# A two-layer graph network on one core: the gathers without memsets, comparisons and one-hot matrices in turn on VectorE, and the last table in four banks

## The chip, the core and the metric

The kernel runs on one core of a Trainium2 chip. Its engines are called by the profile's names: PE (TensorE, the matrix engine; PEld is its weight load), DVE (VectorE), ACT (ScalarE), POOL (GpSimd) and SP (SyncE). [...] An indirect DMA, which fetches rows by a list of indices, is issued by POOL.

The metric is device microseconds (us) of one execution, the median of the runs shown.

## The reference

`x` has 12500 nodes of 128 features. 200000 edges go from `src` to `dst`, sorted by `dst`, and each has one of 8 types. Two layers are computed, each of the form

```
W    = einsum("rb,bio->rio", comp, basis)        # one 128x128 matrix a type
msgs = einsum("ni,rio->nro", x, W)[src, et]      # a message an edge
mean = segment_sum(msgs, dst*8 + et) / max(count, 1)   # mean a node and type
h    = relu(mean.sum over types + x @ root + bias) + x
```

and the output is `layernorm(x + h)` after the second layer, row by row. All of it is float32.

## The kernel before, in words

**Tiles and batches.** The sorted edges are cut into 1563 tiles of 128 edges. Eight tiles make a batch (the code's `q`, `o` or `g`; 196 batches a layer, the last with 3 tiles). For every tile POOL issues one indirect gather (line 645) of 128 rows of 512 bytes: rows of `x` in the first layer (`l == 0`), rows of the table `y_d` in the second. The rows of a batch land in one of `AHEAD + 2` = 7 buffers (`rows_r`, line 556); gathers are issued 5 batches ahead of their use.

**First layer.** For each tile, `onehot` (line 964) writes a 128x128 matrix `dm` on DVE: 1/count where a column is the edge's place (node and type, `kr`), 0 elsewhere (line 979, 8 instructions a batch, which read `cols` in PSUM). `means` (line 1047) multiplies the gathered rows by `dm` on PE (line 1055); float32 matmuls appear twice in the profile, so a batch has 16. `take_means` copies the result to SBUF on ACT, `product` (line 1076) applies the 8 type matrices (line 1084), `place` (line 1096) adds the result to the right nodes by another one-hot matrix `pl` (made at the end of `onehot`, line 987), and `finish` (line 1123) adds bias and root term, the relu and the residual. Each finished block of 128 nodes is then multiplied by the second layer's type matrices (`table`, line 1163, two halves of four types each, bank `pt`) and stored to `y_d`. There are 98 such blocks. The second layer gathers from `y_d`, so it begins when the last table is stored.

**Preparation.** The indices and weights that `onehot` and the gathers use are made during the first 27 batches or so of the first layer, from the edge lists, in groups of four blocks of 128 tiles (`groups`, line 713; the first group is one block and is prepared before the loop). `counts` (line 786) is a generator whose steps are taken two a batch (line 1379): a key; then 47 comparisons of shifted keys on DVE (line 806, float16), four a step, each followed on PE by two counting matmuls into the bank `ct` (lines 812 and 813); then steps for `kr`, the reciprocal of the counts `w` (line 829), `idy` and `near`, each with transposes on PE. The comparisons write into two buffers `eq` in turn, four slots each; a buffer is free again when the counting matmuls that read it are done. `sources` (line 781) makes the gather indices of a later group. `where` (line 855) and checks of the input run in the same place of the loop.

**Order and waits.** `Plan.add` (line 326) takes each piece of work with the cells that it reads and writes, and each engine runs its pieces in the order in which they were added. A piece waits, before its first instruction, for all that its cells need, and its semaphore is raised by its last instruction. In the loop `plan.lazy` is set: a wait for another engine's piece is then moved to the next piece of that engine that already raises a semaphore, if there is one (lines 368 to 370); `means` always raises one (`plan.mark("PE")`).

**Pace of the gathers.** After each of the first 96 gathers POOL runs a memset of 128x256 floats (line 654), and before a memset it waits for the memset two before (line 653).

**End of the first layer.** After the loop the last batches are written out one by one (lines 1421 to 1462). A tile's last halves of tables alternate between `pt` and `ct` for the last two blocks.

Of the kernel before, what the change touches and what calls it, by code (L numbers as in the profile page):

```python
# [422 lines left out]
def ordered_path(  # L423
# [191 lines left out]

    rows_g = {}


    PACE = 2
    rest = keep([P, PACE, 256], F32, "rest")  # L620
    paced = tc.alloc_semaphore("s_paced")
    slow = [0]

    def slower(l, i):
        return 256 if l == 0 and i < 96 else 0

    def gather(l, q):
        if q >= NQ:
            return
        t, cell = rows_r.take()  # L630
        rows_g[l, q] = (t, cell)
        ids = idx if l == 0 else idy

        b = q * Q // P
        reads = [("idy" if l else "idx", b)]
        if l == 0 and q == 0:
            reads = [("idx0", 0), ("idx0", Q // 2)]
        if l == 1 and q == 0:
            reads += [("y_d", j) for j in range(NT - 2)] + [("y_d", j, k) for j in (NT - 2, NT - 1) for k in (0, 1)]

        def some(i0, i1):
            def emit():
                ins = []
                for i in range(i0, i1):
                    ins.append(nc.gpsimd.indirect_dma_start(  # L645
                        out=t[:, i - q * Q, :], out_offset=None, in_=x if l == 0 else y_d,
                        in_offset=bass.IndirectOffsetOnAxis(ap=ids[:, i:i + 1], axis=0)))
                    n = slower(l, i)
                    if n:
                        k = slow[0]  # L650
                        slow[0] += 1
                        if k >= PACE:
                            nc.gpsimd.wait_ge(paced, k - PACE + 1)
                        nc.gpsimd.memset(rest[:, k % PACE, :n], 0).then_inc(paced, 1)  # L654
                return ins

            return emit

        i0, n = q * Q, in_quad(q)
        after = [("done", l)] if q >= NQ - LATE else []  # L660
        if q == NQ - 2:
            for h in range(2):
                plan.add("POOL", some(i0 + h * 4, i0 + h * 4 + 4), reads, [cell + (h,)], lane="gq", n=4, after=after)
        else:
            plan.add("POOL", some(i0, i0 + n), reads, [cell + (0,), cell + (1,)], lane="gq", n=n, after=after)
# [117 lines left out]
        vec(lambda: nc.vector.tensor_copy(t[:, :b1 - b0, :], src_i[:, b0:b1, :]), ends("src", b0, b1), [c])  # L783
        turned("DVE", idx, "idx", t, c, b0, b1, Q if b0 == 0 else 0)

    def counts(i):


        b0, b1 = groups[i]
# [12 lines left out]
        for s0 in range(1, HALO, S4):  # L802
            ss = range(s0, min(s0 + S4, HALO))
            eq, ec = eqs.take()
            for s in ss:
                vec(lambda s=s, eq=eq, s0=s0: nc.vector.tensor_tensor(
                    eq[:, s - s0, :nb, HALO - s:HALO + P], key[:, :nb, HALO - s:HALO + P],
                    key[:, :nb, HALO:HALO + P + s], op=ALU.is_equal), ["key"], [ec + (s - s0,)])

            def emit(ss=ss, eq=eq, s0=s0):  # L810
                for s in ss:
                    nc.tensor.matmul(ct[:, :nb, :], id_h, eq[:, s - s0, :nb, main], start=(s == 1), stop=False)
                    last = nc.tensor.matmul(ct[:, :nb, :], id_h, eq[:, s - s0, :nb, HALO - s:HALO + P - s],
                                            start=False, stop=(s == HALO - 1))
                return last

            pe(emit, [ec + (s - s0,) for s in ss] + ["id_h"], [cc])
            yield
        rel, rc = turns.take()
        vec(lambda: nc.vector.tensor_tensor(rel[:, :nb], dx[:, bs, main],  # L820
# [143 lines left out]
    def onehot(l, q, g=None):  # L964

        if q >= NQ and (g is None or g < 0):
            return
        emits, reads, cells = [], ["cols"], []
        if q < NQ:
            if l == 0:  # L970
                t = dm_t[:, q % 4 // 2, :].rearrange("p (b t c) -> p b t c", b=2, t=Q)[:, q % 2]
                cells += [("dm", q % 4)]
            else:
                t = dm_t[:, q % 2, :].rearrange("p (t c) -> p t c", t=Q)
                cells += [("dm", 2 * (q % 2)), ("dm", 2 * (q % 2) + 1)]
            dms[l, q] = (t, list(cells))
            wide, ids = (P, kr) if l == 0 else (2 * P, near)
            for i in range(q * Q, q * Q + in_quad(q)):
                emits.append(lambda i=i: nc.vector.tensor_scalar(  # L979
                    t[:, i - q * Q, :wide], cols[:, :wide], ids[:, i:i + 1], w[:, i:i + 1], op0=ALU.is_equal,  # L980
                    op1=ALU.mult))
            b = q * Q // P
            reads += [("kr" if l == 0 else "near", b), ("wt", b)]
        if g is not None and g >= 0:
            m = tiles_of(g) * K
            o, c = pl[g] = pl_r.take()
            emits.append(lambda: nc.vector.tensor_scalar(  # L987
                o[:m], cols[:m], pos[:m, g // (2 * R), g % (2 * R):g % (2 * R) + 1], None, op0=ALU.is_equal))
            reads.append("pos")
            cells.append(c)  # L990

        vec(in_turn(emits), reads, cells)
        plan.mark("DVE")

# [49 lines left out]
    def two_blocks(g):  # L1044
        return (g + 1) // 2 - 1

    def means(o):
        t, c = rows_g.pop((0, o))
        d, dc = dms.pop((0, o))
        n = in_quad(o)  # L1050

        def some(i0, i1):
# [4 lines left out]

            return emit

        if o == NQ - 2:  # L1060
            for h in range(2):
                pe(some(4 * h, 4 * h + 4), [c + (h,)] + dc, [s_b[h][1], ("done", 0)])
# [4 lines left out]
    def take_means(o):  # L1067
        n = in_quad(o)
        t, c = sT[o] = sT_r.take()
        for h in range(-(-n // 4)):  # L1070
# [92 lines left out]
    def table(j):  # L1163
# [3 lines left out]
        split = j >= NT - 2  # L1167

        def half(k):
            hb, bc = ct_b if split and k == 1 else pt_b  # L1170

            def first_step():
                pe(lambda: nc.tensor.matmul(hb[:n].rearrange("p r d -> p (r d)"), hT[:, j * P:j * P + n],  # L1173
# [131 lines left out]
    for q in range(AHEAD):  # L1305
        gather(0, q)
    load_x(0)
    run(counts(0), 99)
    sources(*groups[1])
    for h in range(S // 4):  # L1310
        for step in turn_x(0, h):
# [49 lines left out]
    for o in range(NG - 3):  # L1361
# [2 lines left out]
        batch(o)  # L1364
        if o == 1:
            where()
        onehot(0, o + 2, o - 2)
        if not opened:
            end()
# [3 lines left out]
        if o > 0:  # L1373
# [2 lines left out]
                take_product(o - 1)  # L1376
            else:
                late_y.append(o - 1)
        for i in range(2):
            if parts is not None:  # L1380
                if run(parts, 1):
                    parts = None
            elif later:
                later.pop()()
        if o > 2:
            k = place(o - 3)
            close(k)
# [50 lines left out]
    onehot(0, NQ, g - 2)  # L1438
    product(g - 2)
    take_product(g - 2)  # L1440
    while tables:
        table_now()
    placed(g - 2)
    onehot(0, NQ, g - 1)
    onehot(0, NQ, g)
    means(g - 1)
    take_means(g - 1)
    means(g)
    take_means(g)
    product(g - 1)  # L1450
# [4 lines left out]
    placed(g)  # L1455
    now = tables[:]
    tables.clear()
    for h in (0, 2):
        for a, _ in now[h:h + 2]:
            a()  # L1460
        for _, b in now[h:h + 2]:
            b()

    for q in range(AHEAD):
        gather(1, q)
# [94 lines left out]
```

## Time and profile before

| | us |
|---|---|
| median of 3 runs | 3981.41 (3975.88 to 3983.71) |
| the profiled execution | 3979.88 |
| its span, from the first to the last instruction | 3978.1 |
| busy: PE, PEld | 2532.4, 2046.9 |
| busy: DVE, ACT | 1660.6, 390.6 |
| busy: POOL | 2997.6 |
| first gather of the first layer starts | 4.51 |
| first gather of the second layer starts | 2006.07 |
| last memset starts | 149.2 |

The busy times are sums over the whole span; engines work beside each other. POOL's idle time between two gathers stands as "issue" where no other engine ended it. A row of a timeline gives the start and the length of an instruction, or of several alike put together (x8), then the engine, the line, the operation, what it writes and reads, and in brackets how long the engine was idle before it and who ended that. PE's clock, as granted, is given as a share of full speed.

### The profile page before, as it was taken

What the parts mean: (1) busy time and instruction counts of PE and PEld (TensorE: products, weight loads), DVE (VectorE), ACT (ScalarE), POOL (GpSimd) and SP (SyncE); (2) the same over time, 40 slices, a digit from 0 to 9 for tenths busy, and PEclk for the clock granted to TensorE, in tenths of its full rate; (3) what the DMA queues carried; (4) which work ended last, traced back from release to release, by engine and by line L of the source; (5) the groups of instructions that cost most, each with busy time, mean ns of one, the idle gap of its engine ahead of it and who ended that gap; (6) DMA issues with size and microseconds to landing.
All of it is one profiled execution on the core that took longest, in us unless ns stands there. A gap on an engine that the chain in (4) does not pass through costs nothing.

```text
span 3978.1 us, 32124 instructions
## 1 busy us (share of the span) xinstructions
PE 2532.4 (64%) x11213; PEld 2046.9 (51%) x11213; DVE 1660.6 (42%) x4643; ACT 390.6 (10%) x838; POOL 2997.6 (75%) x3230
## 2 busy tenths in 40 slices
PE   6776677776666666667755566555555556555554
PEld 4655555555555555555544444444444444444443
DVE  6566333333333333333234444444444444444443
ACT  1111122221111111111200000000000000000000
POOL 8877777777777777777767777777777777777776
PEclk8897888888888888888877777777777777777777
DMA  3112233332222222222322222222222222222221
GB/s 117 48 52 69 64 106 101 106 95 80 85 85 79 86 85 77 82 80 90 95 68 53 63 53 63 53 64 63 53 63 64 53 63 53 63 64 53 63 58 52
DMA packets 129374, 284.55 MB, mean 72 GB/s; under 512 B 53920, under 2 KB 61356, under 8 KB 129204
## 3 DMA queue, kind: packets, MB, share of 16 engines
q0 software_dynamic: 100032, 205.07, 19.8%
q1 hardware_dynamic: 26122, 75.69, 5.1%
q8 instruction: 90, 1.47, 0.2%
q10 hardware_dynamic: 3049, 1.67, 0.2%
q14 instruction: 81, 0.66, 0.1%
HBM read 223.56 MB, written 58.65 MB: 71 GB/s over the span
## 4 chain that ended last, share of the span: by engine, by line
POOL 74%; issue 23%; PE 2%; DMA 1%; DVE 0%; POOLq 0%; ACT 0%; ACTq 0%; SPq 0%
POOL rows L645 73%; POOL rest L654 1%; PE s L1055 0%; DMA rows<-in_x_dram,idx 0%; PE y L1084 0%; PE pt L1173 0%; PE ct L1084 0%; POOLq L398 0%; PE s L1216 0%; PE po L1115 0%; DVE x_g L1275 0%; DMA y_d<-y_row 0%; DMA rows<-y_d,idy 0%; DMA idx<-in_src_dram 0%; ACT y_row L606 0%
## 5 line engine op out<-in xcount | busy, mean ns | idle before, releaser
L645 POOL DMA_INDIRECT rows<-y_d,idy x1563 | 1476.6, 945 | 495.1 <-issue 495.1
L645 POOL DMA_INDIRECT rows<-in_x_dram,idx x1563 | 1488.2, 952 | 465.0 <-issue 460.0
L979 DVE TENSOR_SCALAR dm<-cols,near,w 128x256 f32<-128x256 f32 x1563 | 724.0, 535 | 1091.5 <-PE s L1216 723.6
L1216 PE MATMUL s<-dm,rows 128*128 128x256 f32 x2086 | 736.7, 522 | 512.7 <-DMA rows<-y_d,idy 489.8
L1216 PEld LDWEIGHTS s<-dm,rows 128*128 128x128 f32 x2086 | 550.5, 274 | 665.6 <-DVE dm L979 268.7
L1055 PE MATMUL s<-dm,rows 128*128 128x128 f32 x3126 | 570.5, 357 | 497.6 <-DMA rows<-in_x_dram,idx 496.6
L1055 PEld LDWEIGHTS s<-dm,rows 128*128 128x128 f32 x3126 | 526.0, 262 | 625.1 <-DMA rows<-in_x_dram,idx 563.0
L979 DVE TENSOR_SCALAR dm<-cols,kr,w 128x128 f32<-128x128 f32 x1563 | 514.7, 401 | 635.9 <-PE s L1055 510.8
L1216 PE MATMUL ct<-dm,rows 128*128 128x256 f32 x1040 | 364.2, 519 | 266.5 <-DMA rows<-y_d,idy 247.5
L1216 PEld LDWEIGHTS ct<-dm,rows 128*128 128x128 f32 x1040 | 272.4, 272 | 342.6 <-issue 140.3
L1084 PE MATMUL y<-w_sb,sT 128*128 128x128 f32 x1824 | 269.7, 311 | 30.8 <-ACT sT L606 30.7
L1084 PEld LDWEIGHTS y<-w_sb,sT 128*128 128x128 f32 x1824 | 261.7, 228 | 37.2 <-ACT sT L606 36.7
L606 ACT ACTIVATE sT<-s 128x512 f32<-128x512 f32 x391 | 213.3, 606 | 204.4 <-PE s L1055 204.3
L1133 DVE TENSOR_TENSOR v<-po,carry 128x128 f32<-128x128 f32 x98 | 28.5, 290 | 483.5 <-PE s L1055 327.5
L606 ACT ACTIVATE y_row<-pt 128x512 f32<-128x512 f32 x196 | 117.1, 597 | 1136.9 <-PE s L1055 1037.0
L1173 PE MATMUL pt<-w_sb,arena 128*128 128x512 f32 x388 | 204.2, 608 | 35.0 <-ACT y_row L606 35.0
L1268 ACT ACTIVATE st<-st,eps 128x8 f32<-128x8 f32 (+1 forms) x13 | 4.0, 308 | 1958.5 <-DVE dm L979 1841.0
L1084 PE MATMUL ct<-w_sb,sT 128*128 128x128 f32 (+1 forms) x1312 | 191.6, 309 | 1.2 <-ACT sT L606 1.2
L1084 PEld LDWEIGHTS ct<-w_sb,sT 128*128 128x128 f32 (+1 forms) x1312 | 188.5, 228 | 1.5 <-ACT sT L606 1.4
L1115 PE MATMUL po<-pl,ys 128*128 128x256 f32 x392 | 117.7, 383 | 0.8 <-DVE pl L987 0.8
L1173 PEld LDWEIGHTS pt<-w_sb,arena 128*128 128x128 f32 x388 | 63.5, 190 | 81.5 <-ACT y_row L606 77.9
L987 DVE TENSOR_SCALAR pl<-cols,pos 128x256 f32<-128x256 f32 x196 | 92.4, 472 | 0.0
(135 smaller groups left out, 1008.0 us busy)
## 6 DMA issues: line engine op xcount, KB each, us to landing
y_d<-y_row SPq DMA_DIRECT2D x96, 512.0 KB, 2.8
rows<-in_x_dram,idx POOLq DMA_INDIRECT x1563, 2.5
rows<-y_d,idy POOLq DMA_INDIRECT x1563, 2.5
x_g<-in_x_dram SPq DMA_DIRECT2D x24, 512.0 KB, 4.6
out_dram<-x_g SPq DMA_DIRECT2D x12, 512.0 KB, 2.7
arena<-in_L_gnn_basis_dram SPq DMA_DIRECT2D x2, 512.0 KB
w_d<-y_row SPq DMA_DIRECT2D x2, 512.0 KB, 2.8
w_sb<-w_d SPq DMA_DIRECT2D x2, 512.0 KB
```

Of the source, the lines that this page charges most:

```text
L606: act(lambda: nc.scalar.activation(out_t, in_t, AF.Copy), reads, writes)
L645: ins.append(nc.gpsimd.indirect_dma_start(out=t[:, i - q * Q, :], out_offset=None, in_=x if l == 0 else y_d, in_offset=bass.IndirectOffset ...
L654: nc.gpsimd.memset(rest[:, k % PACE, :n], 0).then_inc(paced, 1)
L979: emits.append(lambda i=i: nc.vector.tensor_scalar(t[:, i - q * Q, :wide], cols[:, :wide], ids[:, i:i + 1], w[:, i:i + 1], op0=ALU.is_equa ...
L987: emits.append(lambda: nc.vector.tensor_scalar(o[:m], cols[:m], pos[:m, g // (2 * R), g % (2 * R):g % (2 * R) + 1], None, op0=ALU.is_equal))
L1055: last = nc.tensor.matmul(s_b[i // 4][0][:, i % 4, :], t[:, i, :], d[:, i, :], start=True, stop=True)
L1084: last = nc.tensor.matmul(y[:m], t[:, r, :nt, :].rearrange("p t k -> p (t k)"), w_sb[:, 0, r, :], start=(r == 0), stop=(r == R - 1))
L1115: ins = nc.tensor.matmul(a, o[:m], t[:m], start=opens, stop=last and not root_in)
L1133: emits.append(lambda: nc.vector.tensor_add(v[:, :n], a[:, :n], t[:, :n]))
L1173: pe(lambda: nc.tensor.matmul(hb[:n].rearrange("p r d -> p (r d)"), hT[:, j * P:j * P + n], w_sb[:, 1, k * H:(k + 1) * H, :].rearrange("p ...
L1216: ins = nc.tensor.matmul(a, t[:, i, :], d[:, i, :], start=(opens and i == 0), stop=(last and i == n - 1))
L1268: act(lambda: nc.scalar.activation(st[:p, :k, A + M], st[:p, :k, A + 1], AF.Sqrt, bias=eps[:p]), [sc + (1,), "eps"], [sc + (2,)])
```

## The change

Four things are changed, all in the first layer.

- The memsets between the first 96 gathers, their waits, their semaphore and their buffer are gone.
- `counts` no longer puts its comparisons and counting matmuls into the plan at once, but into the lists `between` and `behind` (the first group, prepared before the loop, still does). `onehot` takes the comparisons in `between` and sets each behind one of its own instructions, so that they alternate in one single piece of work of DVE. The counting matmuls in `behind` are added after `product`.
- For this the two preparation steps of a batch are taken ahead of `onehot`, no longer after `product`. The other steps (keys, `kr`, `w`, `idy`, `near`, `sources`, checks) move there as they are, with their transposes.
- At the end of the layer `means` and `take_means` of the last full batch can be done by halves, and a table is put between the halves; the last block's two table halves use the banks of `means` (`s_b`), so that the last two blocks have four banks, and their four matmuls are added before their four copies.

```
-                    n = slower(l, i)
-                    if n:
-                        k = slow[0]
-                        slow[0] += 1
-                        if k >= PACE:
-                            nc.gpsimd.wait_ge(paced, k - PACE + 1)
-                        nc.gpsimd.memset(rest[:, k % PACE, :n], 0).then_inc(paced, 1)
...
-    def counts(i):
+    between, behind = [], []
+
+    def counts(i, alone=False):
...
             for s in ss:
-                vec(lambda s=s, eq=eq, s0=s0: nc.vector.tensor_tensor(
+                one = (lambda s=s, eq=eq, s0=s0: nc.vector.tensor_tensor(
                     eq[:, s - s0, :nb, HALO - s:HALO + P], key[:, :nb, HALO - s:HALO + P],
                     key[:, :nb, HALO:HALO + P + s], op=ALU.is_equal), ["key"], [ec + (s - s0,)])
+                if alone:
+                    vec(*one)
+                else:
+                    between.append(one)
...
-            pe(emit, [ec + (s - s0,) for s in ss] + ["id_h"], [cc])
+            act_on = (emit, [ec + (s - s0,) for s in ss] + ["id_h"], [cc])
+            if alone:
+                pe(*act_on)
+            else:
+                behind.append(act_on)
...
+        for i, (e, r, c) in enumerate(between):
+            emits.insert(2 * i + 1, e)
+            reads += r
+            cells += c
+        between.clear()
         vec(in_turn(emits), reads, cells)
...
-            hb, bc = ct_b if split and k == 1 else pt_b
+            hb, bc = s_b[k] if j == NT - 1 else ct_b if split and k == 1 else pt_b
...
-    run(counts(0), 99)
+    run(counts(0, True), 99)
...
         batch(o)
         if o == 1:
             where()
+        for i in range(2):
+            if parts is not None:
+                if run(parts, 1):
+                    parts = None
+            elif later:
+                later.pop()()
         onehot(0, o + 2, o - 2)
...
-        for i in range(2):
-            if parts is not None:
-                if run(parts, 1):
-                    parts = None
-            elif later:
-                later.pop()()
+        for step in behind:
+            pe(*step)
+        behind.clear()
         if o > 2:
             k = place(o - 3)
...
-    while tables:
+    while len(tables) > 2:
         table_now()
     placed(g - 2)
     onehot(0, NQ, g - 1)
     onehot(0, NQ, g)
-    means(g - 1)
-    take_means(g - 1)
+    means(g - 1, 0)
+    take_means(g - 1, 0)
+    while tables:
+        table_now()
+    means(g - 1, 1)
+    take_means(g - 1, 1)
...
-    for h in (0, 2):
-        for a, _ in now[h:h + 2]:
-            a()
-        for _, b in now[h:h + 2]:
-            b()
+    for a, _ in now:
+        a()
+    for _, b in now:
+        b()
```

More of the change, by code (lines that the diff above doesn't have):

```diff
@@ L616, in ordered_path @@
     rows_g = {}
[L619 to L625, printed above, removed]
     def gather(l, q):
@@ L1045, in two_blocks, with means @@
         return (g + 1) // 2 - 1
-    def means(o):
-        t, c = rows_g.pop((0, o))
-        d, dc = dms.pop((0, o))
+    def means(o, half=None):
+        t, c = rows_g[0, o]
+        d, dc = dms[0, o]
         n = in_quad(o)
@@ L1058, in some @@
             return emit
-        if o == NQ - 2:
-            for h in range(2):
-                pe(some(4 * h, 4 * h + 4), [c + (h,)] + dc, [s_b[h][1], ("done", 0)])
+        if half is not None:
+            pe(some(4 * half, 4 * half + 4), [c + (half,)] + dc, [s_b[half][1], ("done", 0)])
         else:
@@ L1065, in means, with take_means @@
         plan.mark("PE")
-    def take_means(o):
+    def take_means(o, half=None):
         n = in_quad(o)
-        t, c = sT[o] = sT_r.take()
-        for h in range(-(-n // 4)):
+        if o not in sT:
+            sT[o] = sT_r.take()
+        t, c = sT[o]
+        for h in range(-(-n // 4)) if half is None else (half,):
             m = min(4, n - 4 * h)
```

## The prediction

> **What bounds the kernel now.** I read the chain that ended last first, then the instruction groups of the first 450 us, then the timelines of POOL, DVE and PE there. The chain's shares by engine:
>
> ```profile
> POOL 74%; issue 23%; PE 2%; DMA 1%; DVE 0%; POOLq 0%; ACT 0%; ACTq 0%; SPq 0%
> ```
>
> POOL and its own issue time are 97%: 3126 indirect gathers one behind the other, and nothing else matters unless it changes when a gather may start. The groups of the first 450 us (count | busy us, mean ns of one | idle before):
>
> ```profile
> L645 POOL DMA_INDIRECT rows<-in_x_dram,idx x333 | 326.1, 979 | 90.2 <-issue 86.8 <-DMA arena<-in_dst_dram 2.5 <-PE y L1084 0.6
> L654 POOL MEMSET rest<- 128x256 f32 x96 | 31.9, 332 | 0.1
> ```
>
> In the timeline of POOL (start us, duration us) the reader sees a gather every 1.44 us with memsets, one stretched to 3.58, and one every 1.25 us without:
>
> ```profile
> 44.50 0.95 POOL L645 DMA_INDIRECT rows<-in_x_dram,idx  x1 [0.16 <-issue]
> 45.45 0.33 POOL L654 MEMSET rest<- 128x256 f32 x1
> 45.94 3.58 POOL L645 DMA_INDIRECT rows<-in_x_dram,idx  x1 [0.17 <-issue]
> ...
> 157.56 0.94 POOL L645 DMA_INDIRECT rows<-in_x_dram,idx  x1 [0.30 <-issue]
> 158.81 0.94 POOL L645 DMA_INDIRECT rows<-in_x_dram,idx  x1 [0.30 <-issue]
> ```
>
> DVE and then PE in one batch of the preparation (a batch is 8 tiles; o is its number, E(o) the end of its `means` on PE):
>
> ```profile
> 64.17 3.13 DVE L806 TENSOR_TENSOR arena<-arena 128x580 f16<-128x580 f16 x8 [2.54 <-PE s L1055]
> 67.21 2.64 DVE L979 TENSOR_SCALAR dm<-cols,kr,w 128x128 f32<-128x128 f32 x8
> 69.76 0.48 DVE L987 TENSOR_SCALAR pl<-cols,pos 128x256 f32<-128x256 f32 x1
> ```
>
> ```profile
> 62.18 1.95 PE L1055 MATMUL s<-dm,rows 128*128 128x128 f32 x16
> 65.30 2.05 PE L1084 MATMUL y<-w_sb,sT 128*128 128x128 f32 x16 [1.18 <-ACT sT L606]
> 67.19 0.38 PE L812 MATMUL ct<-arena,id_h 128*128 128x512 f16 x1
> ...
> 70.67 0.59 PE L1115 MATMUL po<-pl,ys 128*128 128x256 f32 x2
> 71.10 1.95 PE L1055 MATMUL s<-dm,rows 128*128 128x128 f32 x16
> ```
>
> The comparisons start where `means` ends (64.13); 3.1 us later they are done, just as `product` is, and the 16 counting matmuls (L812, L813) follow without a hole. The one-hot matrices come after, hidden under them. PE's period is 71.10 - 62.18 = 8.9 us, below the 10 us in which POOL gathers 8 tiles.
>
> **The memsets.** 96 gathers go from 1.444 us each (three of them start at 29.61, 31.05 and 32.50) to 1.249 (150.93, 152.18, 153.43): 96 x 0.195 = 18.7 us off POOL's chain, if nothing else holds POOL.
>
> **Stretched gathers.** The mean of 979 ns stands against 945 undisturbed: 333 x 34 ns = 11.3 us, nearly all where L806 runs; the 3.58 us gather lies under one whole run of eight comparisons. [...] I go with the row and leave a third, since a gather can still meet a single comparison (0.4 us): about 8 us saved (0 to 11). With the memsets: 26.6 us.
>
> **The alternation, and the wait it makes.** One-hot matrices and comparisons become one DVE operation: it waits for everything that any part of it needs, and is signalled when its last instruction is done. The comparisons overwrite `eq` buffers that the counting matmuls of the batch before read; as above, that wait is rounded up to E(o). So now the one-hots too start at E(o), and counting waits for all 17 instructions. Their cost is the same rows in another order: 64.17 to 70.24 is 6.1 us (5.8 to 6.3 over the six widths); the next instruction starts 0.08 us before the last one's end at either kind of change, so changing kinds costs nothing. On PE: E(o), 1.2 us for ACT, `product` until 3.05, then idle until 6.2, counting 3.5, `place` 0.5, `means` 1.95, which is E(o+1): a period of 6.2 + 5.95 = 12.1 us, where the row had 8.9. Queued behind the waiting counting matmuls are `place`, table and turn matmuls and the next `means`; for `means` the gather seven batches on waits, since the ring has 7 row buffers.
>
> **The clock in that hole.** PE's idle stretch per batch is now 3.1 us. The same work after such a hole, in PE's timeline, and the clock around it (PEclk is the third number from the end of the window rows):
>
> ```profile
> 47.35 0.61 PE L812 MATMUL ct<-arena,id_h 128*128 128x512 f16 x1 [3.26 <-DVE arena L806]
> ```
>
> ```profile
> 46.40:53.20 6.80, 5.85 (x14) 2.08 (x15) 5.25 (x16) 0.00 (x0) 6.30 (x7) 0.50 0.08 25
> 53.20:104.40 51.20, 40.48 (x264) 29.55 (x263) 32.80 (x90) 6.81 (x15) 45.58 (x70) 1.00 0.17 45
> ```
>
> Of 69 PE holes of 2.6 to 3.6 us in the first layer, 65 are followed by half clock, in the mean for 3.8 us of work: 1.8 us lost. [...] By the trace it is 13.9; I take 13.9.
>
> **How far PE falls behind.** At 10.1 us a batch (8 x 1.249 and 0.1 of stretch) gather q may start at 5.5 + 10.1q, but not before E(q-7). Start: `where` (3.4 us of DVE) and batch 1's sixteen instructions (5.3, no `place` matrix yet) now stand behind the key of group 2, so DVE is done at 42.6 + 3.4 + 5.3 = 51.3, and E(2) = 51.3 + 3.5 + 1.95 + 2.3 of half clock = 59 (before: 55.65). Then 53 preparation steps, two a batch:
> - 16 batches of comparisons (2 to 6, 10 to 15, 19 to 23): 13.85 in the mean, 222 us
> - 2 of `kr` and `w` (7, 16): the 3.35 us reciprocal now stands ahead of `product`: 10.8 each
> - 2 of `idy` and `near`: 7.2 each; one of sources and key: 5.6; one of key and four comparisons: 8.8
>
> E(24) = 59 + 222 + 21.6 + 14.4 + 5.6 + 8.8 = 331 to 332. Gather 31 could start at 318.6: POOL waits 13 us, for the first time. Batches 24 (8.2) and 25 (11.7) give E(26) = 352 against 338.8 for gather 33: still 13. After batch 26 PE needs 6 to 7 us a batch, the lag shrinks and no gather waits again. Directly: gather 33 started at 364.16; now at about 352.1 to 354, depending on how the 3.4 us windows of the clock fall. Worth 10 to 12, say 11 us. Up to batch 20 the wait is covered by the ring's slack (36 us at E(2), near 1 us at E(16)); each further us per comparison batch costs 16 us.
>
> **The other edits.** The last table's four banks spare 0.1 us: its third matmul already started 0.86 us after the second (1998.76, 1999.62), and the fourth waited 0.08 for a copy. `means` of the last full batch in halves moves a table behind its first half; PE is busy there from 1981.30 on, so the sum stays, less up to 0.7 us, plus up to 0.5 where `place` now waits for ACT's copy. Taken as 0 (-0.7 to +0.5). The second layer keeps its instructions.
>
> **Sum.** The profiled execution took 3979.88 us (span 3978.1), 1.5 under the median of 3981.41. 26.6 - 15.6 of waiting (13 and the windows' phase) = 11: 3969 in its terms, **3970.5 as a median**.
>
> **Rivals.** (1) Full gain: PE doesn't fall far enough behind, if holes don't cool the clock (period 12.1, E(24) near 304, before 318.6) or the merged operation starts before E(o). Then 26.6 come through: 3955. For it: no gather waits for a buffer today, and the slack is some 55 us. Against: 16 batches x 2 us of lag at best. (2) Slower: two cold windows per comparison batch, as after 47.35 where counting took 6.35 us for 3.48. That is 1.7 us more for 16 batches, E(24) near 359, past gather 31's old start of 344.11 by 15: 3996. It decides from a period of 14.6 us on; against it, 55 of the 69 holes brought at most a single window. (3) The change does nothing: gathers wait exactly what the memsets took, period 14.6: 3981.
>
> **How the numbers follow.** A measurement here can tell 0.2%, 8 us. Forecast case 0.45 (3962 to 3982; two thirds of it beyond 8 us), full gain 0.25, slower 0.20, nothing 0.10. Faster 0.30 + 0.25, same 0.15 + 0.10, slower 0.20. The range reaches from the full gain with all stretch gone (3951) to near the slower rival: 3952 to 3996.
>
> **What would show it.** Right: no L654; gathers at 1.25 us from the start; one-hots and comparisons alternating from E(o); PE's L812 waiting about 3 us for DVE, at 0.6 us each for the first ones; batches of 13 to 14 us up to about 330 us; POOL idle for 13 to 17 us in all between 290 and 355, released by `means`. Wrong: no idle POOL there (rival 1), or over 30 us of it (rival 2); L806 or L979 longer when alternating; stretched gathers as before.

## The result, and the profile after

The changed kernel took 3971.88 us (median, 3968.67 to 3974.49) against 3982.78 us for the kernel before in the same comparison: a ratio of 0.9973 (95% interval 0.9963 to 0.9983), 10.9 us. The forecast was 3970.5 us, 11 us gained. The size is right; two of the terms that make it are not, and they cancel. The profiled execution took 3973.82 us, its span 3972.0.

The chain that ended last in the changed kernel, its shares by engine (page, part 4):

```profile
POOL 69%; issue 22%; PE 5%; DVE 3%; DMA 1%; ACT 0%; POOLq 0%; ACTq 0%; DVEq 0%; SPq 0%
```

POOL and issue fall from 97% to 91%; 8% now runs through PE and DVE, before it was 2%. Which stretch that is, the groups of the first 450 us tell (count | busy us, mean ns of one | idle before, and what ended it):

```profile
L636 POOL DMA_INDIRECT rows<-in_x_dram,idx x340 | 333.6, 981 | 114.7 <-issue 101.5 <-PE s L1054 9.8 <-DMA arena<-in_dst_dram 2.8
...
L1054 PE MATMUL s<-dm,rows 128*128 128x128 f32 x672 | 84.8, 281 | 7.6 <-DMA rows<-in_x_dram,idx 6.9 <-ACT sT L606 0.7
...
L802 PE MATMUL ct<-arena,id_h 128*128 128x512 f16 x141 | 69.7, 494 | 50.9 <-DVE pl L981 47.9 <-DVE arena L792 3.0
```

The rows of `means` and of counting in the kernel before:

```profile
L1055 PE MATMUL s<-dm,rows 128*128 128x128 f32 x656 | 110.1, 337 | 71.8 <-DMA rows<-in_x_dram,idx 71.0 <-ACT sT L606 0.7
L812 PE MATMUL ct<-arena,id_h 128*128 128x512 f16 x141 | 55.3, 392 | 3.3 <-DVE arena L806 3.3
```

Three readings. The memsets are gone, and POOL waits 9.8 us for `means` (L1054; 8.6 beyond the usual 0.3 of issue at each of four places). `means`, which before stood idle 71.0 us waiting for gathered rows, waits 6.9: PE is now the late one. Counting (L802) waits 47.9 us for the last instruction of the merged DVE operation (L981), and one of its wide matmuls takes 494 ns in the mean instead of 392. And a gather's mean is 981 ns, not below the 979 of before: the stretch of gathers (what they take beyond 0.945 us each), which the prediction took to shrink, is all there. That was one of its signs of being wrong.

The merged operation in DVE's timeline of the changed kernel (start us, duration us, ..., idle before and its releaser):

```profile
62.16 0.41 DVE L973 TENSOR_SCALAR dm<-cols,kr,w 128x128 f32<-128x128 f32 x1 [8.03 <-PE s L1054]
62.48 0.44 DVE L792 TENSOR_TENSOR arena<-arena 128x548 f16<-128x548 f16 x1
62.84 0.40 DVE L973 TENSOR_SCALAR dm<-cols,kr,w 128x128 f32<-128x128 f32 x1
...
67.61 0.47 DVE L981 TENSOR_SCALAR pl<-cols,pos 128x256 f32<-128x256 f32 x1
```

It starts 0.04 us after `means` ends (E(2) = 62.12) and neither kind is longer for alternating: 0.40 us a one-hot, and 0.44 a comparison of 548 elements against 0.45 in the run of eight. PE in the two batches that follow:

```profile
63.29 2.05 PE L1084 MATMUL y<-w_sb,sT 128*128 128x128 f32 x16 [1.17 <-ACT sT L606]
68.14 0.39 PE L802 MATMUL ct<-arena,id_h 128*128 128x512 f16 x1 [2.80 <-DVE pl L981]
...
71.62 1.95 PE L1054 MATMUL s<-dm,rows 128*128 128x128 f32 x16
74.75 2.05 PE L1084 MATMUL y<-w_sb,sT 128*128 128x128 f32 x16 [1.18 <-ACT sT L606]
79.74 0.60 PE L802 MATMUL ct<-arena,id_h 128*128 128x512 f16 x1 [2.94 <-DVE pl L981]
80.12 0.63 PE L803 MATMUL ct<-arena,id_h 128*128 128x512 f16 x1
...
85.33 1.95 PE L1054 MATMUL s<-dm,rows 128*128 128x128 f32 x16
```

Here is the hole that the alternation makes, 2.80 and 2.94 us long. Behind the first PE kept its clock (granted 1.00 from 68.10 to 71.60; 0.39 us each, a batch of 11.45 us from E(2) to E(3)); behind the second it was granted 0.50 for 3.41 us from 79.79 on, eight matmuls took 0.63 us each, counting took 5.15 us instead of 3.48, and the batch took 13.70. Most batches look like the second one. The lag reaches POOL at four places (timeline of POOL, the first gather of batches 29, 30, 31 and 33):

```profile
305.08 0.94 POOL L636 DMA_INDIRECT rows<-in_x_dram,idx  x1 [0.65 <-PE s L1054]
...
319.20 0.94 POOL L636 DMA_INDIRECT rows<-in_x_dram,idx  x1 [3.92 <-PE s L1054]
...
333.23 0.94 POOL L636 DMA_INDIRECT rows<-in_x_dram,idx  x1 [3.62 <-PE s L1054]
...
354.68 0.94 POOL L636 DMA_INDIRECT rows<-in_x_dram,idx  x1 [1.57 <-PE s L1054]
```

At gather 33 the account closes. It started at 364.16 us and now starts at 354.68, 9.5 earlier. Of the memsets' 18.7 us, 8.6 go into waiting (before, no gather waited: the 0.6 us beside PE in its row are the usual issue of two gathers), 0.4 into more stretch and 0.3 into a later first gather: 9.4. Of the 9.5, 7.2 are left where the second layer's first gather starts (1998.92 against 2006.07; 1.9 us go into more stretch of the later gathers, 0.3 into the end of the layer) and 6.1 in the span. Single executions of one kernel lie up to 6 and 10 us apart here, and the medians say 10.9.

### The profile page after: what moved, and what is told of

Read it like the earlier page. It is cut to its first block, busy times and chain, and to the rows that moved or that the text cites. A ratio compares the mean times of both kernels' runs of the same rounds, so it can differ in the third digit from the quotient of the medians.

```text
span 3972.0 us, 32027 instructions
## 1 busy us (share of the span) xinstructions
PE 2527.5 (64%) x11213; PEld 2026.5 (51%) x11213; DVE 1660.1 (42%) x4643; ACT 390.0 (10%) x838; POOL 2969.0 (75%) x3134
## 3 DMA queue, kind: packets, MB, share of 16 engines
q10 hardware_dynamic: 3049, 1.67, 0.2%
## 4 chain that ended last, share of the span: by engine, by line
POOL 69%; issue 22%; PE 5%; DVE 3%; DMA 1%; ACT 0%; POOLq 0%; ACTq 0%; DVEq 0%; SPq 0%
POOL rows L636 69%; DVE dm L973 1%; PE s L1054 1%; DVE arena L792 1%; PE ct L802 1%; PE ct L803 1%; PE y L1084 0%; PE po L1115 0%; DMA w_sb<-in_L_gnn_root_dram 0%; DMA arena<-in_dst_dram 0%; PE pt L1173 0%; DVE arena L823 0%; PE pt L753 0%; ACT sT L606 0%; DVE pl L981 0%
## 5 line engine op out<-in xcount | busy, mean ns | idle before, releaser
L1216 PEld LDWEIGHTS s<-dm,rows 128*128 128x128 f32 x2086 | 549.2, 274 | 673.7 <-DVE dm L973 308.6
L973 DVE TENSOR_SCALAR dm<-cols,kr,w 128x128 f32<-128x128 f32 x1563 | 525.3, 401 | 726.2 <-PE s L1054 597.5
L1054 PE MATMUL s<-dm,rows 128*128 128x128 f32 x3126 | 541.7, 345 | 435.1 <-DMA rows<-in_x_dram,idx 434.4
L1054 PEld LDWEIGHTS s<-dm,rows 128*128 128x128 f32 x3126 | 503.2, 252 | 556.4 <-DMA rows<-in_x_dram,idx 531.1
L802 PE MATMUL ct<-arena,id_h 128*128 128x512 f16 (+1 forms) x188 | 78.3, 437 | 56.3 <-DVE pl L981 47.9
```

What stands on the lines that cost most here:

```text
L973: emits.append(lambda i=i: nc.vector.tensor_scalar(t[:, i - q * Q, :wide], cols[:, :wide], ids[:, i:i + 1], w[:, i:i + 1], op0=ALU.is_equa ...
L1054: last = nc.tensor.matmul(s_b[i // 4][0][:, i % 4, :], t[:, i, :], d[:, i, :], start=True, stop=True)
L1216: ins = nc.tensor.matmul(a, t[:, i, :], d[:, i, :], start=(opens and i == 0), stop=(last and i == n - 1))
```

## The experiments

The theory after this reading has three parts. Removing the memsets is worth their whole price. The alternation saves nothing on gathers, and costs what POOL waits for row buffers. That wait comes from the hole in PE's work together with the half clock behind the hole. The rivals: the alternation itself saves time and something else eats it; or the lag of PE is only the longer DVE operation, with or without the clock.

### Four runs in which POOL is not the bound

The first four kernels ran on a chip on which the kernel before then took 4741.55 us. Their expectations:

> The kernel before without its memsets, everything else as it was: comparisons in runs of eight, one-hot matrices after them. Theory (the new wait eats the gain): the old order keeps PE at 8.9 us a batch, no gather ever waits for a buffer, so the memsets' 18.7 us come through whole: 3964 (3961 to 3968), idle POOL beyond the issue gap under 1 us in the first layer. Rival A (the memsets shielded the gathers from the runs of comparisons): gathers are stretched by 25 us or more in the first 340 instead of 11.8, and the time is 3975 or above. Rival B (the alternation is what gains): 3980 or above.

> The changed kernel with the 96 memsets and their waits put back. Theory: PE runs as late as in the changed kernel (batches of 13.5 to 14 us, end of means 24 near 333), but POOL itself comes later, so it hardly waits (0 to 2 us); the stretch is about the same 12 us: 3983 (3979 to 3987), as before the change. Rival A (alternation alone saves stretched gathers): under 3977. Rival B (the late PE costs on its own): above 3989.

> The changed kernel with 8 row buffers in place of 7. Theory: a gather then waits for the means eight batches back, 10 us more slack than the 8.6 us that POOL waits in the changed kernel: no idle POOL in the first layer, PE as late as before (means 24 ends near 333): 3963 (3960 to 3967). Rival (the idle time only shows up elsewhere, or the saving goes to more stretch): 3969 to 3974, as the changed kernel.

> The changed kernel with 12 more matmuls (float16, zeros, added to the counts) between product and counting in 15 of the batches, 2.6 us at full clock, so that PE is not idle while it waits for VectorE. Theory (hole and clock): counting then starts at full clock, a batch takes 12.1 to 12.4 us and not 13.8, means 24 ends near 308, no gather waits: 3963 (3960 to 3967). Rival (the clock is no part of it, VectorE alone sets the batch): batches stay at 13.5 to 14 and the time at 3972. Rival B (the extra matmuls delay counting): batches over 14 us, above 3975.

Measured against the kernel before: 1.0001 (0.9955 to 1.0046), 0.9969 (0.992 to 1.0017), 1.0036 (0.9996 to 1.0076) and 1.0009 (0.9964 to 1.0054). Nothing is told apart. The reason is in the page of the first of them (without memsets): the chain, and the group of gathers of the first layer, whose third number is the idle time before them.

```profile
another core or an unknown queue 46%; PE 24%; DVE 17%; issue 8%; ACT 4%; DMA 0%; DVEq 0%; ACTq 0%; SPq 0%
...
L637 POOL DMA_INDIRECT rows<-in_x_dram,idx x1563 | 1489.2, 953 | 979.5 <-issue 443.2
```

The same kernel where the kernel before takes the usual time, same row of the page:

```profile
L637 POOL DMA_INDIRECT rows<-in_x_dram,idx x1563 | 1492.3, 955 | 478.5 <-issue 474.5
```

A gather costs POOL the same in both, but in the long runs POOL stands idle 501 us more in the first layer, and the chain runs through work that the records give no name to. The transfers are not slower: they end 2.2 us after the gather's start in both traces (median, from the DMA packets; signals of landing are not in the traces of the long runs). It is PE and DVE that stop, for 9 to 22 us at a time, as early as in the preparation of the first group. The row of its counting matmuls in the first 120 us of the long run:

```profile
L797 PE MATMUL ct<-arena,id_h 128*128 128x128 f16 x47 | 10.3, 300 | 71.9 <-issue 46.7 <-DVE arena L791 25.2
```

In the usual run this row has 5.2 us of idle time. So E(0) came at 103.35 us instead of 39.29, and eight gathers start 12.6 us apart in the mean, in place of 10.0. Nothing that makes POOL quicker can show where POOL is not what ends last. What stops PE and DVE there was not found. Nor is it shown to belong to the chip: the record numbers it 3, and so it does the chip of a later comparison in which the kernel before took 3979.16 us. The same kernels were therefore run again; all that follows, but for one run that is named, is from comparisons in which the kernel before took 3977.65 and 3979.16 us.

### Without memsets, old order

```diff
-                    n = slower(l, i)
-                    if n:
...
-                        nc.gpsimd.memset(rest[:, k % PACE, :n], 0).then_inc(paced, 1)
```

> The kernel before without its memsets, again, on a chip where a gather lands 2.5 us after its issue as in the profile of before (on the last chip 8 gathers landed only every 11.9 us in the mean, so that POOL was not the bound and no variant could differ: ratios 0.997 to 1.004). Theory as before: PE keeps 8.9 us a batch, no gather waits for a buffer, 18.7 us come through: ratio 0.9953 (0.9945 to 0.9963). Rival A (gathers need the memsets): stretch of 25 us or more, ratio above 0.998. If this chip is like the last one: ratio 0.998 to 1.002 and POOL idle all through the first layer.

3961.50 us, ratio 0.9957 (0.994 to 0.9974), 16 us. No gather waits for a row buffer, batches take 8.5 to 9.1 us at the start, and gather 33 starts at 349.10, 15.1 us earlier than in the kernel before. What is missing of 18.7 is stretch: up to gather 33 the gathers take 15.0 us beyond their pace of 1.444 and 1.249 us here, against 11.2 before. So the memsets are worth their price, less a loss that no step of the prediction had. Taking them out without the other edits looks at least as good as the whole change (0.9957 against 0.9973), but the two were measured in different comparisons and their intervals overlap.

### The alternation alone, memsets kept

```diff
+                    n = slower(l, i)
+                    if n:
...
+                        nc.gpsimd.memset(rest[:, k % PACE, :n], 0).then_inc(paced, 1)
```

> The changed kernel with the 96 memsets and their waits put back, on a chip with the usual landing time. Theory: alternation does not spare stretched gathers (12.6 us in the changed kernel, 11.8 before), and with the memsets POOL is itself so late that the late PE costs it 0 to 2 us: ratio 1.000 (0.9988 to 1.0012). Rival A (alternation gains by itself): below 0.9985. Rival B (the late PE costs by itself, whatever POOL does): above 1.0015.

3979.28 us, ratio 0.9999 (0.9989 to 1.0009). The groups of its first 450 us:

```profile
L644 POOL DMA_INDIRECT rows<-in_x_dram,idx x332 | 327.0, 985 | 89.8 <-issue 86.6 <-DMA arena<-in_dst_dram 2.4 <-PE y L1099 0.3
L653 POOL MEMSET rest<- 128x256 f32 x96 | 32.2, 336 | 0.0
```

A gather takes 985 ns in the mean, 979 before, and the stretch of the first 340 gathers is 13.5 us against 11.8. The order of the comparisons saves nothing. POOL waits for no row buffer: E(24) is as late as in the changed kernel (332.36 against 332.96), but with memsets the gathers come late too.

### One more row buffer

```diff
-    rows_r = Ring(const, AHEAD + 2, [P, Q, D], F32, "rows")
+    rows_r = Ring(const, AHEAD + 3, [P, Q, D], F32, "rows")
```

> The changed kernel with 8 row buffers in place of 7, again. Theory: the 8.6 us that POOL waits in the changed kernel vanish, PE stays as late (means 24 ends near 333): ratio 0.995 (0.9942 to 0.996), as without memsets alone. Rival: the idle time moves elsewhere, ratio 0.9973 as the changed kernel. On a chip like the last one: 0.998 to 1.004.

3961.97 us, ratio 0.9958 (0.9941 to 0.9974). PE is as late as ever (E(24) = 329.45, batches of 13.7 to 14 us), and POOL does not wait at all; gather 33 starts at 347.94. The group row of POOL has no wait but the usual ones:

```profile
L636 POOL DMA_INDIRECT rows<-in_x_dram,idx x345 | 340.6, 987 | 107.5 <-issue 103.6 <-DMA arena<-in_dst_dram 2.6 <-PE s L1054 1.2
```

(The 1.2 are 0.3 of issue at four gathers.) So a late PE costs nothing that shows here by itself; its price passes through the ring of seven buffers.

### Work for PE in the hole

```diff
+        if len(behind) == 2 and not fresh:
+            def fill():
+                for _ in range(12):
+                    last = nc.tensor.matmul(ct_b[0], id_h, nil, start=False, stop=False)
+                return last
+
+            pe(fill, ["id_h", "nil"], [ct_b[1]])
         for step in behind:
             pe(*step)
```

Twelve matmuls with a matrix of zeros stand ahead of the counting matmuls in 15 batches: more work for PE, none of it needed.

> The changed kernel with 12 more matmuls of zeros ahead of counting in 15 batches, again. Theory (hole and clock): batches of 12.1 to 12.4 us in place of 13.8, means 24 ends near 308, no gather waits: ratio 0.995 (0.9942 to 0.996). Rival (the clock is no part of it): batches stay at 13.5 to 14, 0.9973. Rival B (counting comes later): batches over 14, above 0.998.

3959.11 us, ratio 0.9951 (0.9934 to 0.9968). PE's timeline in one batch of it:

```profile
82.91 2.05 PE L1087 MATMUL y<-w_sb,sT 128*128 128x128 f32 x16 [1.17 <-ACT sT L606]
84.80 2.75 PE L1392 MATMUL ct<-nil,id_h 128*128 128x512 f16 x12
88.05 0.39 PE L803 MATMUL ct<-arena,id_h 128*128 128x512 f16 x1 [0.50 <-DVE pl L984]
88.28 0.38 PE L804 MATMUL ct<-arena,id_h 128*128 128x512 f16 x1
```

Counting starts no earlier after `product` than before, but at 0.38 us each from its first matmul on. Most batches take 11.8 to 12.4 us, E(24) is 307.07 instead of 332.96, POOL waits 0, gather 33 starts at 346.02. This parts the two causes: with the same late signal, but counting at 0.38 us each, no gather waits.

### The merged operation in two pieces

```diff
+        if len(between) > 4:
+            front = []
+            for one, (e, r, c) in zip(emits[:4], between[:4]):
+                front += [one, e]
+            vec(in_turn(front), reads + between[0][1], cells + [x for _, _, c in between[:4] for x in c])
...
+            del emits[:4], between[:4]
+            cells = []
```

> The changed kernel with the alternating operation of VectorE cut in two pieces of four one-hots and four comparisons, each with its own signal, so that the first half of the counting starts when the first piece is done. Theory (one signal for 17 instructions is what opens the hole): PE's idle stretch goes from 3.1 to about 1.4 us, which does not halve the clock, a batch takes 10.3 to 10.8 us, PE falls behind by 8 us or less over the preparation, no gather waits: ratio 0.995 (0.9942 to 0.996). Rival (the start at the end of means is what counts, not the signal): batches of 12 or more, 0.9973.

3960.95 us, ratio 0.9955 (0.9938 to 0.9972). The order on DVE is the same, but the first four comparisons are signalled on their own. PE:

```profile
69.71 0.38 PE L802 MATMUL ct<-arena,id_h 128*128 128x512 f16 x1
...
72.81 0.39 PE L802 MATMUL ct<-arena,id_h 128*128 128x512 f16 x1 [1.20 <-DVE pl L992]
...
74.99 1.95 PE L1065 MATMUL s<-dm,rows 128*128 128x128 f32 x16
```

The first half of counting follows `product` without a hole, a hole of 1.20 us is left before the second, the clock holds (0.38 and 0.39 us a counting matmul), and most batches take 9.7 to 10.7 us; E(24) = 275.9, POOL waits 0. The hole came from one signal for seventeen instructions, not from the alternation.

### What stretches a gather

The gathers of the changed kernel under the alternation, and the two-input comparisons of the same microseconds (timelines of POOL and DVE):

```profile
321.69 1.12 POOL L636 DMA_INDIRECT rows<-in_x_dram,idx  x1 [0.30 <-issue]
323.12 1.18 POOL L636 DMA_INDIRECT rows<-in_x_dram,idx  x1 [0.30 <-issue]
324.60 1.19 POOL L636 DMA_INDIRECT rows<-in_x_dram,idx  x1 [0.30 <-issue]
```

```profile
321.50 0.50 DVE L792 TENSOR_TENSOR arena<-arena 128x672 f16<-128x672 f16 x1
...
322.98 0.50 DVE L792 TENSOR_TENSOR arena<-arena 128x680 f16<-128x680 f16 x1
...
324.47 0.50 DVE L792 TENSOR_TENSOR arena<-arena 128x688 f16<-128x688 f16 x1
```

Each gather starts while a comparison runs and ends 0.82 us after that comparison: 322.00 + 0.82 = 322.82, the gather ends at 322.81; 323.48 gives 324.30, as measured; 324.97 gives 325.79, as measured. The 3.58 us gather of the kernel before follows the same sum. The run of eight that it lies under:

```profile
45.85 2.85 DVE L806 TENSOR_TENSOR arena<-arena 128x516 f16<-128x516 f16 x8
```

45.85 + 2.85 + 0.82 = 49.52 = 45.94 + 3.58. But this gather is an exception, and the prediction took it for the rule. Two gathers start under the run of eight that the prediction shows, from 64.17 to 67.30 (chain of the kernel before, in order of time):

```profile
64.67 1.16 POOL rows L645
66.32 1.03 POOL rows L645
```

Neither is held to the end of the run. The first starts under the run's second comparison, which ends at 65.01, and 65.01 + 0.82 = 65.83 = 64.67 + 1.16. In the kernel before, comparisons make 29 of the first 340 gathers late by more than 30 ns, 8.3 us in all; 27 of them are held by one comparison, and only two by several (2.6 and 0.8 us). The old order without memsets has three such, 5.6 us, which is why its stretch is larger. Why some gathers don't get in between two comparisons of a run, the runs do not show.

In the alternation no gather is held by more than one comparison, but more gathers meet one: 52 of the first 340, 8.5 us in all. A pair of one-hot and comparison takes 0.74 us, two of them 1.48, and a held gather with its issue 1.43 to 1.48, so that the gathers fall into step with the comparisons: all 36 gathers of the changed kernel that follow a held one in the same operation are late too. With what other instructions hold, 73 of the first 340 gathers are late in the changed kernel, 12.0 us in all; in the kernel before 46, 11.0 us.

This is how regular it is over the six traces with the alternation and these comparisons. Of 296 gathers that start while a comparison runs and has over 0.14 us left, 295 end within 0.015 us of 0.82 us after it. Of those that start ahead of a comparison next to none waits for it (5 of some 530 such meetings).

To test this, `split` was run with every comparison of two slices in SBUF replaced by one of constants in PSUM (`cols`; the kernel keeps the outputs of its matmuls there too) with 1.0, over as many elements:

```diff
-                one = (lambda s=s, eq=eq, s0=s0: nc.vector.tensor_tensor(
-                    eq[:, s - s0, :nb, HALO - s:HALO + P], key[:, :nb, HALO - s:HALO + P],
-                    key[:, :nb, HALO:HALO + P + s], op=ALU.is_equal), ["key"], [ec + (s - s0,)])
+                one = (lambda s=s, eq=eq, s0=s0: nc.vector.tensor_scalar(
+                    eq[:, s - s0, :nb, HALO - s:HALO + P], cols[:, None, :P + s].to_broadcast([P, nb, P + s]),
+                    1.0, None, op0=ALU.is_equal), ["key", "cols"], [ec + (s - s0,)])
```

> The kernel with the alternating operation in two pieces, in which each comparison of two SBUF tensors is replaced by a comparison of PSUM columns with a constant, of the same number of elements; the counts are therefore not computed, the rest is. Theory (a gather that reaches its read while a comparison with two SBUF inputs runs waits for the end of that comparison): the stretch in the first 340 gathers falls from 14.4 to 5 us or less and none lies under a replaced comparison; no gather waits for a buffer; 9 to 10 us below the two-piece kernel: ratio 0.993 (0.9918 to 0.9942). Rival (the stretch comes from a busy VectorE or from transfers): 12 us or more of stretch, ratio 0.9955.

The stretch of the first 340 gathers falls from 14.4 us in `split` to 4.0, and no gather under a replaced comparison is late. This takes both inputs out of SBUF, not one. One alone was not tried on the comparisons; the nearest case is line 1133, a `tensor_tensor` of one tensor in PSUM and one in SBUF: over nine traces 82 gathers start under it, and none ends 0.82 us after it. Nor does any of 69 that start under the long reciprocal of one SBUF tensor. But gathers were held under an instruction without two SBUF inputs as well: all 12 that start under the `tensor_scalar` of 128x896 int32 (line 798 before), with one SBUF input, end 0.82 us after it.

The time was missed: 3975.53 us, ratio 0.9991 (0.9981 to 1.0001). The replaced instruction is longer, and that brings back the wait. DVE, then POOL, then POOL's group in the first 450 us of this kernel:

```profile
203.57 0.41 DVE L975 TENSOR_SCALAR dm<-cols,kr,w 128x128 f32<-128x128 f32 x1 [3.99 <-PE s L1065]
203.90 0.78 DVE L792 TENSOR_SCALAR arena<-cols 128x612 f16<-128x612 f32 x1
```

```profile
208.70 0.94 POOL L636 DMA_INDIRECT rows<-in_x_dram,idx  x1 [0.30 <-issue]
...
220.51 0.94 POOL L636 DMA_INDIRECT rows<-in_x_dram,idx  x1 [4.63 <-PE s L1065]
```

```profile
L636 POOL DMA_INDIRECT rows<-in_x_dram,idx x337 | 321.9, 955 | 126.9 <-issue 99.4 <-PE s L1065 24.5 <-DMA arena<-in_dst_dram 2.5
```

0.78 us in place of 0.47 for 612 elements makes most batches 12 to 14.8 us: gathers at an even 0.94 us, mean 955, and 24.5 us of waiting for `means`. The ring takes more than the gathers save.

One more run tried the replaced comparison where nothing else is merged with it, in the kernel before without memsets.

> The kernel before without its memsets (3961.5 us when it ran alone, gathers stretched by 15.1 us among the first 340, no wait for row buffers), with every comparison of two key slices replaced by a comparison of the constant columns in PSUM with 1.0: same partitions, same elements, same output, but no SBUF input. The counts are not computed, so the output is not the reference's. Theory (a two-input comparison holds the gather that starts under it): with one input the stretch falls to 5 us or less, as it did in one_input (4.0); here the comparisons don't stand in one operation with the one-hot matrices, the batches stay below 10.5 us and POOL waits for no row buffer, so the saving shows in the time: 10 us off 3961.5, ratio to before 0.993 (0.9915 to 0.9945), gather 33 at 340 us against 349.1. Rival (the stretch moves to other instructions, or what it takes is given back later in the layer): stretch over 10 us or the ratio stays at 0.9955 to 0.996.

It ran where the kernel before took 4670.67 us, as in the first four runs: ratio 1.002 (0.9982 to 1.0057), which says nothing of POOL's time. Its trace does say something of the stretch: 3.8 us over the first 340 gathers, where the same order with two-input comparisons had 11.4 in the first four runs; of these about 8 us lay under comparisons, and no gather that meets only replaced comparisons and one-hot matrices is late now. Both times the cause is confirmed and its worth in time is not measured; the 8 to 11 us of stretch under comparisons are the most that it could be.

### Comparisons further apart

`split` with one preparation step a batch instead of two from batch 9 on, and two one-hot matrices between comparisons:

```diff
-            emits.insert(2 * i + 1, e)
+            emits.insert(gap * i + gap - 1, e)
...
-        for i in range(2):
+        for i in range(2 if o < 9 else 1):
```

> The two-piece kernel, with one preparation step a batch in place of two from batch 9 on, so that two one-hots stand between two comparisons (the preparation ends near batch 45; tables start at batch 64 and not 42, and the second product bank is used from batch 56 on). Theory (a gather that was held starts its next read 1.25 us after the comparison's end; with pairs of 0.72 us it then meets the next comparison but one, with 1.05 us for two one-hots and a comparison it mostly meets a one-hot): the stretch of groups 2 and 3 falls by half or more, in all from 14.4 to 9 us, no gather waits for a buffer: ratio 0.9942 (0.993 to 0.9952). Rival (stretch only depends on the number of comparisons): 13 us or more, 0.9955.

3960.52 us, ratio 0.9955 (0.9938 to 0.9971). The stretch fell from 14.4 to 10.7 (31 gathers late under comparisons instead of 56), less than expected, and gather 33 started at 343.35 instead of 348.31, but the time is that of `split`. The stretch can be thinned out; 5 us at gather 33 did not show in the median, and the profiled spans (3958.5 against 3961.6) are single executions.

Four versions, `fill`, `split`, `sparse` and the one without memsets in the old order, at 0.9951 to 0.9957, are ahead of the kernel before, as is the larger ring at 0.9958. In all five gather 33 starts 5.6 to 11.3 us earlier than in the changed kernel, but their intervals overlap its 0.9963 to 0.9983, and they were not measured beside it. Their order among each other is not resolved.

## Why the prediction was right, and where it was not

**The memsets, 18.7 us.** Right. Without them 15.1 us arrive at gather 33 and the rest is in the gathers' stretch.

**Stretched gathers, 8 us saved.** Wrong, and the one step that failed outright. That a comparison holds a gather was read rightly (295 of 296 end 0.82 us after it). But the 3.58 us gather is not what the mean of 979 ns is made of. Comparisons hold 8.3 of the 11.8 us, not nearly all, and holds by several of them, the part that the alternation takes away, are 3.4. The prediction left a third for gathers that meet a single comparison; 4.8 us of that kind were there already, and they became 8.5, since 52 gathers are late by a comparison now where 29 were. The stretch is 12.6 us after, 11.8 before, and 13.5 with the alternation alone. The range was 0 to 11: no trace of the kernel before shows its lower end, and the runs of this change lie just beyond it, with no saving at all. How much of the stretch comes with the comparisons shows in `split` and `one_input`: 14.4 us, against 4.0 with no comparison input in SBUF.

**The merged operation waits for E(o) and signals at its end.** Right: it starts 0.04 us after `means`, and PE's hole before counting is 2.7 to 3.3 us (once 1.0, once 4.1) where 3.1 was forecast. `split` shows that the single signal makes it.

**Half clock, a period of 13.9 and not 12.1.** Right. The 16 batches took 217 us (222 forecast), 13.6 in the mean; `fill` has 12.3 where the hole is covered. The forecast is 12.1, the sum at full clock, and the 1.8 us lost behind a hole. Here the holes of the trace (65 of 69 followed by half clock) decided the case: at 12.1 us a batch E(24) would have been about 304 by the prediction's sum, and `fill`, with 307.07, has no gather that waits.

**How far PE falls behind.** Nearly right: E(2) = 62.12 (59 forecast; the merged operation of batch 1 ended at 54.13, not 51.3), E(24) = 332.96 (331 to 332), E(26) = 354.40 (352). Gather 33 at 354.68 lies just past the 352.1 to 354 forecast.

**POOL's wait, 13 to 15.6 us.** Wrong in size: 8.6, and it began at batch 29, not 31. This is the stretch again. Had the gathers been 8 us quicker, gather 31 would have stood at its buffer at 318.6; without the waits it would in fact have come at 325.9 (333.23 less the 7.3 waited until then), so PE was less far behind it. Where POOL ends up waiting, the gather starts when `means` lets it, however early POOL was: 8 us less saved, 7 us less waited. That is why the total survived the failed step: 11 forecast, 9.5 at gather 33, 10.9 in the medians.

**The other edits, 0.** Not resolved. From the last gather's end to the first of the second layer it is 19.19 us before and 19.50 after; the variants, some of which have these edits and some not, have 17.65 to 20.26.

**The rivals.** The full gain did not come. Where no gather waits for PE it is 0.9951 to 0.9958, some 16 to 19 us, and never 26.6, since the stretch stays. The slower case needed two steps of the clock (3.41 us each in the traces) at half of it in each batch; counting took 5.15 us for 3.48, 1.67 lost, which is one. That the gathers would wait for exactly what the memsets took is refuted by the changed kernel itself: they wait 8.6 of 18.7 us.

## What to carry to other kernels

When an edit takes time off the engine that bounds a kernel, work out batch by batch when the next engine comes late, and count a saving ahead of such a wait as nothing: it only lengthens the wait, here by 8.6 of 18.7 us. Merging two operations to change their order also merges their waits and their signals; signal the pieces on their own, as in `split`, where the order is the same and POOL waits 0. Count how many instructions meet a holder, times what is left of it: here the same comparisons, spread over more time, met 52 gathers instead of 29, and the sum did not fall (8.5 us after 8.3). And before one striking row is taken for the rule, see how the other rows in the same place end.

## What the runs showed of the hardware

In the six traces with the alternation, 295 of the 296 gathers that start under a comparison (a `tensor_tensor` of two SBUF slices) with over 0.14 us left of it end 0.82 us after it; an undisturbed gather takes 0.94 to 0.95 in all. In back-to-back runs of three to eight comparisons, 60 of 68 gathers (kernel before, and without memsets) still get in behind the comparison under which they started; five of the rest were held up to 2.4 us longer. Of 82 gathers that start under line 1133, a `tensor_tensor` with one input in PSUM, none is held.

In the kernel before, first layer, half clock followed stretches in which PE was idle for most of the time, not only those without any work. In steps of 3.41 us (all of its clock records start whole multiples of that apart): of 125 steps at full clock in which PE was busy less than about 45%, 124 were followed by half clock, and in some 100 of them PE had worked for part of the step; of 270 over 55%, none; in between, 4 of 12. Back from half clock, all 125 steps over about 85% were followed by full clock and none of 39 below 75%. From these counts an estimate for the changed kernel: a hole of 2.9 us is 85% of such a step, so that at most of its positions it leaves one step under 45% busy. Behind the hole at 76.80 the half clock lasted one step, 3.41 us; twelve useless matmuls in the hole (`fill`) bought up to 1.7 us a batch, 1.3 in the mean of sixteen.

The same gathers cost POOL the same (953 and 955 ns) where the kernel before takes 4.67 to 4.74 ms as where it takes 3.98. In the long run without memsets the first `means` ends 64 us later, because PE and DVE stop for 9 to 22 us at a time, while the transfers of the rows end as soon after their gathers. The cause is open, and one chip number stands on both sides, so an edit is to be measured beside the kernel before, each time.
